# Side work between scores and maxima, and reciprocals on transposed blocks, in a two-layer attention and expert kernel

## The chip, the cores and the metric

The kernel runs on one core of one Trainium2 chip. The metric is the device time of one execution in microseconds (us); a comparison takes the median of several executions. The engines are named as in the profile: PE (TensorE; its weight loads are PEld), DVE (VectorE), ACT (ScalarE), POOL (GpSimd) and SP (SyncE, which only starts transfers here).

## What is computed

The reference is a stack of two layers on an input of 8 batches of 1024 rows of 128 numbers. Each layer has attention and then a mixture of experts, each behind a normalisation. Only the attention of layer 0, and the routing that prepares the experts of layer 0, are touched by the change:

```python
# layer 0: attention with 8 heads of 32, keys and values through a latent of 64
q = (x @ Wq.T).reshape(b, t, 8, 32)
kv_latent = x @ Wkv_down.T
k = (kv_latent @ Wk_up.T).reshape(b, t, 8, 32)
v = (kv_latent @ Wv_up.T).reshape(b, t, 8, 32)
scores = jnp.einsum('bqhd,bkhd->bhqk', q, k) * 32 ** -0.5
attn = jax.nn.softmax(scores, axis=-1)
out = jnp.einsum('bhqk,bkhd->bqhd', attn, v).reshape(b, t, 256) @ Wo.T
# layer 0: 14 experts of width 256, each row goes to its best two
probs = jax.nn.softmax(rows @ gate_w.T, axis=-1)
top2_p, top2_i = jax.lax.top_k(probs, 2)
...
```

Layer 1 (causal linear attention with 16 heads, 8 experts of width 512, one expert for each row) follows and is the same in both kernels.

## The kernel before

**Stages.** In the profiled execution the attention of layer 0 takes the time from about 52 us (first scores) to 1246 us. The experts of layer 0 follow until about 1423 us, then layer 1 until the end.

**Tiling.** The 8 heads are taken in two groups of 4, so there are 16 pairs n of batch and group. Each pair is cut into two blocks of 512 queries; there are 32 blocks. A block is worked off in 8 chunks of 128 keys (`kc`), and each chunk in two half steps (`hp` 0 and 1; `h` counts half steps over the whole stage). So there are 256 chunks.

**One chunk.** In the half step `hp` 0, `scores` makes the transposed scores of one chunk of keys for 512 queries and 4 heads: for each head a small matmul puts minus the row maximum into a bank of PSUM (line 398), the matmul of keys and queries adds the scores (line 399), and ACT takes the exponential of the bank (line 402). In the half step `hp` 1, `largest` makes untransposed scores of a later block (`LEAD` is 24 half steps, so 12 chunks ahead) for 4 heads (line 359), and DVE takes the negated maximum of each bank (line 363). `weigh` multiplies the exponentials of the chunk before with the values (line 414); it comes as two halves of 256 queries, one in each half step, except in the last chunks.

**Row sums.** The sums of the exponentials are gathered by POOL: it adds pairs of exponential tiles (line 228, a helper through which all pinned POOL work goes), and adds them into the tile `total`, partly by transfers that accumulate. Eight half steps after the end of a block, `add_up` sums `total` over the partitions with a matmul (line 424). `settle` then copies the sums to SBUF on ACT (line 435), and in eight pieces of 64 columns, one in each half step, DVE takes reciprocals (line 440) and POOL multiplies the weighed values with them (`outT<-nums,dens`).

**Maxima to rows.** `spread` reduces the maxima of a block (line 371), `spread_rows` transposes them on PE (line 376), splits them into three bf16 parts on DVE (lines 379 to 382) and sends them with 12 small transfers on SP's queue to the places where `scores` reads them.

**Banks.** All these matmuls but those of `weigh` write to one pool of 7 PSUM banks (`a_big`). A new tile takes the bank that came free first, in the order of the program. `weigh` has a bank of its own.

**Side work.** Between the two halves of the main work stand pieces for other batches: normalisation (`Norm`: `stats`, `power`, `offset`, `scaled`, `turned`), projections to queries and keys (`project`), `values`, and for finished batches `Finish`: the output projection, a normalisation, the routing `logits`, the steps of the choice of two experts (`first` to `weights`), `count` and `rank` of the rows, and `places`, after which 16 indirect transfers of each batch move its rows to the experts' regions (line 620, on POOL's queue). Lists give each piece its half step (`at(h, ...)`, in the dictionary `todo`). A piece stands behind the scores or the maxima of its half step, and in front of the half weighing:

```python
for piece in todo.pop(h):
    piece()
if weighing is not None:
    ...
        weigh(*weighing, half=hp)
```

**Order.** PE, DVE and ACT run their instructions in exactly the order in which the program issues them (`manual_schedule`), and POOL's pinned instructions as well. An engine that waits holds up all that stands behind it.

## Time and profile before

| what | value |
|---|---|
| median of 3 executions | 1997.78 us (1995.19 to 2002.73) |
| profiled execution, its own time | 2006.14 us |
| span of its trace, first to last instruction | 2003.8 us |
| mean granted PE clock | 0.964 |
| attention of layer 0 in the trace | about 52 to 1246 us |
| busy in 52 to 1246 us | PE 1166 us, DVE 896 us, POOL 905 us, ACT 665 us |

In a row of the groups, the name behind the line and the engine is the operation, then the tile written and the tiles read with their shapes, the number of instructions, and behind the bar the time in which at least one of them ran and the mean duration of one in ns. The last part is the time in which the engine idled in front of them, and what it waited for. A row of the timeline gives the start, the length, and how many instructions of a kind it merges (x8); in square brackets stands idle time in front of it. Matmuls of several heads overlap, so a merged row is longer than the distance to the next row's start; costs on PE are therefore taken from start to start. A row of windows gives the stretch, its length, then the busy time of PE, PEld, DVE, ACT and POOL, the granted clock and the DMA share.

### The profile page before, as it was taken

The page shows a single profiled execution, that of the slowest core. Times are in us where ns is not written, and L with a number is a line of the kernel's source. Part 1 is how long each engine was busy: PE and PEld are TensorE (multiplying, and loading weights), DVE is VectorE, ACT ScalarE, POOL GpSimd, SP SyncE. Part 2 cuts the span into 40 slices and gives each one's busy share as a digit, 9 for nine tenths or more (in the row PEclk, how much of TensorE's full clock was granted, in tenths as well). Part 3 has the DMA queues.
Part 4 walks back from the last instruction along what each step waited for, and adds up shares of the span by engine and source line. Part 5 has one row for each costly group of instructions (what it writes and reads, how often), then busy time and mean ns, then how long its engine had stood idle before and what let it go on. Part 6 is the DMA issues. An engine that isn't in the chain of part 4 may idle for free. (4 is left out here: it accounts for less than half of the span.)

```text
span 2003.8 us, 46295 instructions
## 1 busy us (share of the span) xinstructions
PE 1914.5 (96%) x17765; PEld 1010.4 (50%) x17765; DVE 1385.9 (69%) x3551; ACT 1083.1 (54%) x2338; POOL 1287.2 (64%) x1403
## 2 busy tenths in 40 slices
PE   8999999999999999999999998999599999998997
PEld 3333333333333333333333333699467777765897
DVE  6577778778778778778767785467457777754454
ACT  3455565564654565565565553366457666641443
POOL 1568668877778778778777884432545666624465
PEclk9999999999999999999999998999789999987999
DMA  5335345344344344444434441344222211101332
GB/s 154 64 79 108 70 86 110 71 95 100 83 92 102 83 88 99 91 88 96 93 78 102 98 96 72 135 132 134 81 71 87 79 50 51 51 23 54 108 106 63
DMA packets 64387, 176.41 MB, mean 88 GB/s; under 512 B 14889, under 2 KB 33776, under 8 KB 52512
## 3 DMA queue, kind: packets, MB, share of 16 engines
q0 software_dynamic: 30656, 136.45, 30.0%
q1 hardware_dynamic: 30112, 28.97, 5.2%
q10 hardware_dynamic: 3392, 7.95, 1.3%
q8 instruction: 143, 2.34, 0.5%
q14 instruction: 84, 0.69, 0.1%
HBM read 42.08 MB, written 35.96 MB: 39 GB/s over the span
## 5 line engine op out<-in xcount | busy, mean ns | idle before, releaser
L363 DVE TENSOR_REDUCE nmp<-big 128x1 f32<-128x512 f32 x1024 | 632.6, 680 | 248.9 <-PE big L359 248.8
L402 ACT ACTIVATE e<-st 128x512 f32<-128x512 f32 x1024 | 530.2, 603 | 379.3 <-PE st L399 303.8
L228 POOL TENSOR_TENSOR e<-e 128x512 f32<-128x512 f32 x364 | 452.3, 1288 | 8.1 <-PE num L414 7.8
L399 PE MATMUL st<-qT,kT 32*128 32x512 f32 x2048 | 340.6, 597 | 0.0
L414 PE MATMUL num<-e,v 128*32 128x256 f32 (+1 forms) x4040 | 332.0, 400 | 0.4 <-issue 0.3
L359 PE MATMUL big<-kT,qT 32*128 32x512 f32 x2048 | 320.1, 651 | 0.0
L414 PEld LDWEIGHTS num<-e,v 128*32 128x32 f32 x4040 | 81.1, 108 | 335.1 <-issue 304.6
L228 POOL TENSOR_TENSOR outT<-nums,dens 128x64 f32<-128x64 f32 x248 | 96.0, 510 | 168.2 <-DVE nm L371 99.5
L228 POOL TENSOR_TENSOR total<-e 128x512 f32<-128x512 f32 x124 | 154.7, 1320 | 46.3 <-ACT e L402 45.8
L1168 POOL DMA_INDIRECT got<-rows_out,found x128 | 125.8, 983 | 89.2 <-PE tp L1203 43.7
L399 PEld LDWEIGHTS st<-qT,kT 32*128 32x128 f32 x2048 | 154.8, 194 | 38.5 <-issue 33.0
L398 PE MATMUL st<-nb,ones_h 3*128 3x512 bf16 x1024 | 149.1, 389 | 11.0 <-DVE nmp L363 8.1
L359 PEld LDWEIGHTS big<-kT,qT 32*128 32x128 f32 x2048 | 102.1, 185 | 110.9 <-issue 46.9
L620 POOL DMA_INDIRECT rows_in<-xn,at x128 | 130.5, 1019 | 31.4 <-issue 30.9
L440 DVE RECIPROCAL dens<-dens 128x64 f32<-128x64 f32 x248 | 126.7, 531 | 4.5 <-ACT dens L435 4.5
L1717 POOL DMA_INDIRECT out_x<-y,to x72 | 79.1, 1098 | 67.4 <-DVE y L1715 53.4
L228 POOL DMA_DIRECT2D total<-e x91 | 84.4, 927 | 43.3 <-POOL e L228 23.9
L1698 ACT ACTIVATE g<-ph,wt 128x256 f32<-128x256 f32 x144 | 63.6, 474 | 85.3 <-PE ph L1695 85.3
L1016 POOL DMA_DIRECT2D rows_out<-y x68 | 39.4, 580 | 96.8 <-DVE y L1013 85.2
L398 PEld LDWEIGHTS <-ones_h 3*128 3x128 bf16 x1024 | 33.6, 91 | 128.3 <-issue 124.6
L1129 POOL TENSOR_TENSOR rs<-ve,mhalf 128x2 f32<-128x2 f32 x64 | 46.2, 722 | 80.1 <-DVE ve L1127 62.6
L1223 ACT ACTIVATE qm<-qk,cst 128x256 f32<-128x256 f32 x128 | 54.6, 496 | 53.6 <-DVE qk L1220 45.4
(289 smaller groups left out, 3064.5 us busy)
## 6 DMA issues: line engine op xcount, KB each, us to landing
total<-e POOLq DMA_DIRECT2D x91, 1024.0 KB
xr<-rows SPq DMA_DIRECT2D x36, 257.0 KB
xr<-rows_in SPq DMA_DIRECT2D x72, 128.0 KB
rows_out<-y POOLq DMA_DIRECT2D x68, 128.0 KB
nb<-part SPq DMA_DIRECT2D x384, 1.0 KB
blob<-in_blob ACTq DMA_DIRECT2D x8, 578.0 KB
blob<-in_blob SPq DMA_DIRECT2D x14, 321.0 KB
x<-in_x SPq DMA_DIRECT2D x8, 512.0 KB
```

The source lines that it names most:

```text
L228: return tc.keep_in_program_order(f(*args, **kw))
L359: nc.tensor.matmul(ps, lhsT=qTs[n][r, qc * P:(qc + 1) * P], rhs=kTs[n][r, kb * BLK:(kb + 1) * BLK], start=True, stop=True,)
L363: nc.vector.tensor_reduce(nmps[n][:, h, qc, kb:kb + 1], ps, AX.X, ALU.max, negate=True)
L398: nc.tensor.matmul(st, lhsT=ones_h[r3, :], rhs=nbs[n][r3, cols], start=True, stop=False)
L399: nc.tensor.matmul(st, lhsT=kTs[n][r, kc * P:(kc + 1) * P], rhs=qTs[n][r, cols], start=False, stop=True)
L402: nc.scalar.activation(e[:, h, :], st, AF.Exp, scale=SCALE0)
L414: nc.tensor.matmul(nums[n, qb][32 * h:32 * h + 32, cols], lhsT=vs[b][:, kc, c0:c0 + HD0], rhs=e[:, h, cols], start=kc == 0 and half != 1, ...
L440: nc.vector.reciprocal(s[:, cols], s[:, cols])
L620: ins = nc.gpsimd.indirect_dma_start(out=rows_in, out_offset=bass.IndirectOffsetOnAxis(ap=ats[k][:, j:j + 1], axis=0), in_=xn[:, c0 + j, : ...
L1168: ins = tc.keep_in_program_order(nc.gpsimd.indirect_dma_start(out=gots[p][:, i, k, :], out_offset=None, in_=rows_out, in_offset=bass.Indir ...
L1698: nc.scalar.activation(g[:, k, :], ps, AF.Relu, bias=w[:, L_B1 + k:L_B1 + k + 1])
L1717: ins = nc.gpsimd.indirect_dma_start(out=out_rows, out_offset=bass.IndirectOffsetOnAxis(ap=at[:, i:i + 1], axis=0), in_=y[:, i, :], in_off ...
```

## The change

1. The side work is divided in two: products of PE (`product`, in the dictionary `beside`) stand in the half step `hp` 0, behind the scores and in front of the maxima; what is left for DVE from them is run behind the maxima of the same chunk (`behind_maxima`). The functions `spread_rows`, `Finish.project`, `logits` and `rank` return their DVE part for this. ACT copies of projections, values and transposes stay with the product.
2. In a chunk with such a product, `weigh` comes as a whole behind the maxima; in the others it stays halved.
3. The half steps of all pieces are written anew (`frame`, `complete`, `last_half`); the output projection of a batch comes in 4 pieces of 2 chunks instead of 2 of 4; `places` is cut in two; the row sums come 11 half steps after the end of a block instead of 8.
4. `settle` no longer copies the sums. DVE transposes their 32x32 blocks straight from PSUM, takes 16 reciprocals for each partition, and transposes them back from a broadcast; POOL multiplies all 512 columns at once.
5. Two small copies of `counts` go from DVE to ACT for whole batches.

In the built order of the changed kernel, `counts<-ahead` stands on ACT in front of the exponentials of the next chunk.

```diff
         def spread_rows():
             ...
             nc.tensor.transpose(ps[:4 * CPK, :P], nm.rearrange("p h c -> p (h c)"), ident)
+            return lambda: spread_parts(n, qb, ps)
+
+        def spread_parts(n, qb, ps):
             parts = [stat0.tile([4 * CPK, P], BF16, name=f"part{i}") for i in range(3)]
...
-        def settle(n, qb, pieces):
+        def settle(n, qb):
...
-            out_b, top = outs[b, 0], tops.pop(0)
-            s = work.tile([P, BLK], F32, name="dens", bufs=1)
-            nc.scalar.copy(s, dens.pop((n, qb)))
-            w = BLK // pieces
-
-            def divide(i):
-                cols = slice(i * w, (i + 1) * w)
-                nc.vector.reciprocal(s[:, cols], s[:, cols])
+            out_b, top, den = outs[b, 0], tops.pop(0), dens.pop((n, qb))
+            few = stat0.tile([P, BLK // 32], F32, name="few")
+
+            def invert():
+                turned = work.tile([P, BLK // 32, 32], F32, name="dens", bufs=1)
+                nc.vector.transpose(turned.rearrange("p c d -> p (c d)"), den)
+                nc.vector.reciprocal(few, turned[:, :, 0])
+
+            def divide():
+                s = work.tile([P, BLK // 32, 32], F32, name="dens", bufs=1)
+                nc.vector.transpose(s, few.unsqueeze(2).to_broadcast([P, BLK // 32, 32]))
                 ins = pinned(
-                    nc.gpsimd.tensor_tensor,
-                    out_b[:, g, qb * BLK + i * w:qb * BLK + (i + 1) * w], top[:, cols], s[:, cols], ALU.mult,
+                    nc.gpsimd.tensor_tensor, out_b[:, g, qb * BLK:(qb + 1) * BLK], top,
+                    s.rearrange("p c d -> p (c d)"), ALU.mult,
                 )
...
+                self.copy = nc.scalar.copy if n == CPB else nc.vector.tensor_copy
...
-                nc.vector.tensor_tensor(xv, ps, xv, ALU.add)
+                return lambda: nc.vector.tensor_tensor(xv, ps, xv, ALU.add)
...
-                nc.vector.tensor_copy(self.both[:, :, 0], counts)
+                self.copy(self.both[:, :, 0], counts)
...
-                nc.vector.tensor_copy(counts, ahead[:, :, CPB])
+                self.copy(counts, ahead[:, :, CPB])
...
+        def frame(f):
+
+            h0 = 2 * CPB * 4 * f
+            if 1 <= f < NB - 1:
+                projections(2 * f + 1, h0, (0, 1, 4, 2))
+            if f == NB - 2:
+                projections(2 * f + 3, h0, (24, 26, 28, 30))
+            b = f + 2
+            if b < NB:
+                for i, k in enumerate((15, 16, 17, 23)):
+                    at(h0 + 2 * k + 1, measure, b, i)
+                at(h0 + 49, lambda b=b: prepared[b].power())
+            b = f + 1
+            if 2 <= b < NB:
+                at(h0 + 3, start_norm, b)
+                at(h0 + 3, lambda b=b: prepared[b].offset())
+                for i, k in enumerate((3, 4, 5, 6)):
+                    at(h0 + 2 * k + 1, lambda b=b, i=i: prepared[b].scaled(2 * i))
+                product(h0 + 14, turn_both, lambda b=b: prepared[b])
+                projections(2 * b, h0, (8, 11, 12, 14))
+                for i, k in enumerate((15, 17, 19, 25)):
+                    product(h0 + 2 * k, values, b, i)
+            if f:
+                complete(f - 1, h0)
+
+        def complete(b, h0):
+
+            f, norm = Finish(b, 0, CPB), []
+            for i, k in enumerate((3, 6, 9, 10)):
+                product(h0 + 2 * k, f.project, 2 * i, 2)
+            at(h0 + 13, lambda: norm.append(f.norm()))
+            for i, k in enumerate((7, 8, 10, 11)):
+                at(h0 + 2 * k + 1, lambda i=i: norm[0].stats(2 * i))
+            at(h0 + 23, lambda: norm[0].power())
+            at(h0 + 27, lambda: norm[0].offset())
...
+            product(h0 + (30 if last else 32), turn_both, lambda: norm[0])
+            product(h0 + (32 if last else 36), f.logits)
+            steps = (
+                (39, f.first), (39, f.exponentials), (45, f.second), (49, f.third), (51, f.fourth),
+                (51, f.exponential2), (53, f.count), (65, f.place, 0), (67, f.place, 1), (69, f.softmax),
+                (71, f.weights),
+            )
...
+        def settle_soon(h, n, qb):
+            invert, divide = settle(n, qb)
+            at(h + 1, invert)
+            at(h + 2 + h % 2, divide)
+
+        def summed(h, n, qb, e):
+            add_up(n, qb, e, True, True)
+            settle_soon(h, n, qb)
...
                     elif not quiet:
                         smax_step(h + LEAD)
-                    if spreading and h % HALVES == (HALVES + 1 - LEAD) % HALVES:
-                        spread_rows()
+                        for piece in behind_maxima:
+                            piece()
+                        behind_maxima = []
+                    if spreading and h % HALVES == (HALVES - LEAD) % HALVES:
+                        behind_maxima.append(spread_rows())
+                    products = beside.pop(h)
+                    if hp == 0:
+                        split = not products
+                    for piece in products:
+                        behind_maxima.append(piece() or (lambda: None))
...
-                        else:
+                        elif quiet or split:
                             weigh(*weighing, half=hp)
+                        elif hp == 1:
+                            weigh(*weighing)
...
-                                due[h + 8] = n, qb, total
+                                product(h + 11, summed, h + 11, n, qb, total)
```

## The prediction

> **What bounds the kernel now.** I read the page first (shares, slices), then the groups, then one frame by windows, then single chunks by the timeline. The page and two groups:
>
> ```profile
> span 2003.8 us, 46295 instructions
> PE 1914.5 (96%) x17765; PEld 1010.4 (50%) x17765; DVE 1385.9 (69%) x3551; ACT 1083.1 (54%) x2338; POOL 1287.2 (64%) x1403
> ...
> DVE  6577778778778778778767785467457777754454
> ...
> PEclk9999999999999999999999998999789999987999
> ...
> L363 DVE TENSOR_REDUCE nmp<-big 128x1 f32<-128x512 f32 x1024 | 632.6, 680 | 248.9 <-PE big L359 248.8
> ...
> L440 DVE RECIPROCAL dens<-dens 128x64 f32<-128x64 f32 x248 | 126.7, 531 | 4.5 <-ACT dens L435 4.5
> ```
>
> TensorE (PE) looks full, but its 96% hides waits: matmuls overlap, and one head of four that starts late costs time in a "busy" engine. Attention is 256 chunks from 52 to 1246 us, 4.66 us each; only it changes. The timeline of PE in a chunk without side work, then in a stalled one:
>
> ```profile
> 647.48 0.41 PE L398 MATMUL st<-nb,ones_h 3*128 3x512 bf16 x4
> 647.71 1.05 PE L399 MATMUL st<-qT,kT 32*128 32x512 f32 x8
> 648.69 0.64 PE L414 MATMUL num<-e,v 128*32 128x256 f32 x8
> 649.26 1.34 PE L359 MATMUL big<-kT,qT 32*128 32x512 f32 x8
> 650.52 0.64 PE L414 MATMUL num<-e,v 128*32 128x256 f32 x8
> 651.10 0.43 PE L398 MATMUL st<-nb,ones_h 3*128 3x512 bf16 x4
> ...
> 629.02 0.41 PE L398 MATMUL st<-nb,ones_h 3*128 3x512 bf16 x3
> 629.25 1.04 PE L399 MATMUL st<-qT,kT 32*128 32x512 f32 x6
> 631.52 0.37 PE L398 MATMUL st<-nb,ones_h 3*128 3x512 bf16 x1 [1.23 <-DVE nmp L363]
> ...
> 634.29 2.09 PE L359 MATMUL big<-kT,qT 32*128 32x512 f32 x8
> ```
>
> Start to start, scores take 1.21 us, each half of the weighing 0.57, maxima 1.26: 3.61. In the second chunk three heads of the scores start (x3) and the fourth 2.5 us later: it waits for a bank that VectorE (DVE) frees by a maximum. PE then loses its clock (maxima 2.09 long for 1.19) and the chunk takes 8.30. On DVE stood:
>
> ```profile
> 601.67 1.23 DVE L540 TENSOR_TENSOR cand<-cand,cst 128x112 f32<-128x112 f32 x1
> 602.83 0.54 DVE L440 RECIPROCAL dens<-dens 128x64 f32<-128x64 f32 x1
> 603.29 2.41 DVE L363 TENSOR_REDUCE nmp<-big 128x1 f32<-128x512 f32 x4
> ...
> L571 DVE COPY both<-counts x9: 160/619/2992, 314.0 to 1254.3; 128x14 f32<-128x14 f32 x9
> ```
>
> Between two sets of maxima lie routing steps and reciprocals; a copy of 14 elements takes 0.16 to 2.99 us, by what POOL does. So the bound is PE plus waits for banks. I call 32 chunks (64 half steps) a frame, k = 0 to 31. By windows, frame 4 is
>
> ```profile
> 637.00:788.00 151.00, 148.83 (x1292) 55.68 (x1288) 115.51 (x251) 85.82 (x170) 118.80 (x126) 0.99 0.44 92
> ```
>
> (PE, weight loads, DVE, ACT, POOL: DVE 76%, POOL 79%). Frames 1 to 5 run from 182.84 to 938.75 (first scores to first scores in the timeline), 151.2 us each. PE's own pieces of a frame, each without a wait, are 32 x (1.21 + 1.07) for scores and maxima, 36.0 for 64 half weighings, 26.1 for side work: 135. Some 16 us are waits, 9 of them in k = 20 to 31 (routing steps on DVE).
>
> **Part 1: side work between scores and maxima, weighing whole behind them.** A whole weighing in the tail takes 1.00 us (1204.78 to 1205.79) for 2 x 0.57: 0.14 saved where it is whole, 24 chunks of a frame, 3.3 us. But the banks (7, given out in the order in which they come free) set a new wait. With a side bank a chunk asks for 9, and its fourth maximum takes the bank of the second score. Exponentials begin 1.35 after the scores (647.48, first exponential 648.83), the first takes 0.60, the next end 0.48 later each: the second ends at +2.43. Maxima could start at 1.21 + 1.06 (a projection, 643.16 to 644.22) = +2.27, so they wait 0.2, as the plain chunk does for its first exponential (1.26 for 1.07). Kinds of chunk in the changed order:
> - 18 with one piece of about 1.05 us (6 projections, 4 values, 4 output projections of two chunks instead of 2 of four at 1.98, 4 row sums): 1.21 + 1.05 + 1.27 + 1.00 = 4.53; 81.6.
> - 2 with both transposes, 2 with spread transpose and projection (10 banks; the third exponential is waited for): 5.0 each; 20.1. Logits 1.21 + 1.81 + 1.07 + 1.00 = 5.09. Rank 0.63, waiting to +2.48: 4.55.
> - 2 with the spread transpose alone, weighing still halved, maxima waiting 0.5: 1.21 + 0.21 + 0.57 + 1.57 + 0.57 = 4.13; 8.3. 6 plain: 3.62; 21.7.
> Sum 141.3. Pieces drained by DVE are now drained behind the maxima, so the next scores wait for the second maximum instead of the first: 12 x 0.1 net = 1.2. That makes 142.5. What is late next is thus ACT's second exponential, no longer DVE.
>
> **Part 2: reciprocals.** Out: 8 x 0.46 (start to start) = 3.7 us of DVE per block of 8 chunks, ACT's copy of the sums (31 x 0.585 = 18 us, hidden in ACT's 46% idle), POOL's 8 products (96.0/31 = 3.1 us) and POOL's waits for them (168 us in all; hidden too, since POOL holds up exponentials for 13.6 us in all). In: two transposes of 128x512, one reciprocal 128x16 (0.2 by the 128x8 row, 203 ns), one POOL product 128x512 (1.28, as e<-e). The trace has no DVE transpose. Nearest rows: the 512-wide reduction, 0.60 start to start, and tensor_tensor 128x512, 0.69. I take 0.65. Ends: 0.60, and 2.4 (four bytes in four passes); nothing below[...]. So 1.5 for 3.7, in one place per block, behind the maxima of the chunk with the row sums. The gap that DVE has there until the next maxima is about 4.3 us from set to set, less 4 x 0.60: 1.9 on average (1.6 in front of a plain chunk), so 1.5 fits.
> At this place a rule could speak against the change. The row: the 128x14 SBUF copy takes 0.16 at best, 1.53 in the mean of frames 2 to 6, POOL being busy. If the second transpose (SBUF to SBUF) is held up so, 31 x 1.0 us come late, some 30 us, and the gain is gone. The Trainium skill, "SBUF — State Buffer", § Who interferes with whom, lists copy, cast and tensor_scalar as ops that take the port pair shared with GpSimd, and says that a DVE op with at most one SBUF input outside the 2-port modes does not contend. It doesn't name the transpose. I take the rule's zero, and keep 30 us for the range.
>
> **Part 3: routing, counts, moves.** The sums come 3 half steps later (11 for 8), so PE's waits for the landing of total (weighing 2.59 long at 134 us, 2.25 at 465) go. Routing steps are spread over more chunks. Left: the third step, 0.67 + 1.23 behind a plain chunk's maxima, where 3.6 less 4 x 0.60 leaves 1.2, so 0.7 too long; with others 1.0 per frame. The two copies of counts go to ACT (DVE 1.5 + 0.3 saved), but ACT is in order: counts<-ahead waits for the scan, which stands behind the maxima of k = 26 and the pair sum; it ends about 2.9 us into k = 27, whose exponentials, due at 1.35, queue behind it; the maxima wait for them: 1.9 per frame. Also off is moved from half step 26 to 27, in front of ACT's scaling in the same half step: the exponentials of k = 14 come 1.0 late: 1.0. The 16 indirect moves of a frame keep their pace (one per 4 half steps) and start 7 half steps later; on POOL they and the e sums pass one product instead of 8, and that product stands behind a full set of e sums (5 us), by when its transpose is done. Costed at nothing, hidden by POOL's 21% of slack; if that were gone, the place would cost POOL 1.3 for 3.1, still no loss. SP's 12 spread DMAs per block follow the same DVE steps, three and a half chunks before their use: nothing, and before that cover is gone they would have to land 15 us later.
> Frame: 142.5 + 1.0 + 1.9 + 1.0 = 146.4, for 151.2: -4.8, times 5 = -24. Frame 0 (130.4, no projections): -2. Frame 6 (153.4; four more pieces in k = 24 to 30, 3.7): -3. Frame 7 to the tail (86.8, by the same kinds 83.6): -3. Tail: -1. **Sum -33.** The profiled execution took 2006.1 (2003.8 in the span), so 1973; it lies 8 over the median 1997.8, so **1965**.
>
> **Rivals.** (a) Larger gain, about 1938: the 0.2 before each side chunk's maxima (18 x 0.2 x 6 = 22) doesn't appear, nor part of the ACT waits. For: before, chunks with side work had maxima of 1.07, no wait. Against: half a weighing stood there too.
> (b) No change, about 1994: ACT's late exponentials pass on to the next chunks (bank, maxima, DVE), 4 more per frame, or a second transpose held by POOL. For: the stall at 629 shows how one late DVE step takes two chunks and the clock.
> (c) Slower, 2039: transposing 4-byte values takes DVE several passes. At 2.0 us each the steps need 2 x 2.0 + 0.3 in a gap of 1.9: 31 x 2.4 = 74 lost, less 33, so 1998 + 41. It decides from 31 x (2T + 0.3 - 1.9) = 33, T = 1.3 us. For: no row. Against: DVE's other 512-wide ops are at 0.7.
> (d) That the change doesn't do what it says: the built order has one side piece in front of the maxima in 24 of 32 chunks and whole weighings behind, so no.
>
> **How the numbers follow.** 0.5% (10 us) is about what a measurement can tell from no change. Forecast 0.54 (own range 1948 to 1983), (a) 0.17, (b) 0.14, (c) 0.15: faster 0.71, same 0.14, slower 0.15. The range goes from half of (a) over (b): 1932 to 2006.
>
> **What would show it.** Right: 31 transposes of each kind at 0.6 to 0.7, RECIPROCAL 128x16 near 0.2; num matmuls 128x512 in three of four chunks; side chunks of 4.5 with maxima of 1.27; PE's waits on nmp gone from k = 20 to 31; an ACT wait of 2 us at counts<-ahead; PEclk without dips before 1180. Wrong: transposes over 1.3; scores over 2 us after each side chunk; side chunks of 4.33 (then (a)).

## The result: 9.5% slower, and the profile after

The changed kernel takes 2190.16 us (median of 4 runs, 2183.14 to 2195.32) where the kernel before takes 2000.25 on the same chip: a ratio of 1.095, 95% interval 1.090 to 1.100. The forecast was 1965 us, range 1932 to 2006. The profiled execution took 2195.29 us. From its page, then its groups of DVE:

```profile
span 2193.4 us, 43466 instructions
PE 2009.3 (92%) x16493; PEld 1032.1 (47%) x16493; DVE 1404.8 (64%) x3396; ACT 1066.0 (49%) x2321; POOL 1251.3 (57%) x1186
...
DVE  6565666767667767667666766457645767763454
...
PEclk9998999999998998899899997899968999996999
...
L363 DVE TENSOR_REDUCE nmp<-big 128x1 f32<-128x512 f32 x1024 | 636.3, 684 | 423.9 <-PE big L359 422.5
```

```profile
L297 DVE SCALAR_TENSOR_TENSOR off<-mv,rs 128x8 f32<-128x8 f32 (+1 forms) x18 | 33.8, 1877 | 1.8 <-POOL rs L228 1.8
L446 DVE STREAM_TRANSPOSE dens<-few 128x512 f32<-128x512 f32 x31 | 22.0, 711 | 1.0
L441 DVE STREAM_TRANSPOSE dens<-den 128x512 f32<-128x512 f32 x31 | 21.9, 706 | 0.0
L442 DVE RECIPROCAL few<-dens 128x16 f32<-128x16 f32 x31 | 7.9, 254 | 1.1
```

The transposes are close to what they were taken for (0.71 us for 0.65), so the way to a slower kernel that the prediction named is not the one taken. All engines are busy for a smaller share of the span than before; the clock row has its dips all over attention; DVE idles longer in front of the maxima (422.5 us for 248.8), waiting for PE. And one row stands out: `off`, a 128x8 step, takes 1877 ns on average, where the same line took 96 ns in attention before. A chunk with one piece of side work came out as forecast to the hundredth of a us. PE in one, by the timeline:

```profile
642.96 0.41 PE L401 MATMUL st<-nb,ones_h 3*128 3x512 bf16 x4
...
644.17 1.13 PE L334 MATMUL val<-wv_sb,xT 128*128 128x256 f32 x4
645.23 1.34 PE L359 MATMUL big<-kT,qT 32*128 32x512 f32 x8
646.49 1.07 PE L417 MATMUL num<-e,v 128*32 128x512 f32 x8
647.49 0.41 PE L401 MATMUL st<-nb,ones_h 3*128 3x512 bf16 x4
```

Start to start: scores 1.21, values 1.06, maxima 1.26, weighing 1.00, together 4.53 as forecast. The loss sits in a few chunks of each frame. (Chunk k is counted within the frame, k = 0 to 31, as in the list of half steps.) The windows' row of one frame, k = 0 to 31:

```profile
546.34:720.15 173.81, 158.98 (x1101) 57.35 (x1099) 121.34 (x230) 83.22 (x168) 115.34 (x99) 0.92 0.39 80
```

173.8 us for 151 before. Over an undisturbed chunk of their kind, k = 4 takes 5.6 us more, k = 14 7.6, k = 20 4.1, k = 27 6.6, k = 0 1.5 (up to 8.5 in other frames), and six more together 5.5. Without these 30.9 us the frame is 142.9; the prediction's sum without waits was 142.5. So the plan held, and the waits were missed. Three of them by the timeline, first k = 14 (DVE, POOL, PE and ACT):

```profile
621.60 4.93 POOL L228 TENSOR_TENSOR e<-e 128x512 f32<-128x512 f32 x4
621.68 4.88 DVE L297 SCALAR_TENSOR_TENSOR off<-mv,rs 128x8 f32<-128x8 f32 x1
622.84 1.12 PE L359 MATMUL big<-kT,qT 32*128 32x512 f32 x2
626.49 0.70 DVE L441 STREAM_TRANSPOSE dens<-den 128x512 f32<-128x512 f32 x1
626.60 0.88 ACT L310 ACTIVATE xn<-x,off,rs 128x128 f32<-128x128 f32 x2 [7.65 <-DVE off L297]
627.34 3.23 PE L359 MATMUL big<-kT,qT 32*128 32x512 f32 x6 [3.37 <-DVE dens L441]
```

`off` starts 0.08 us after POOL began four additions, and ends when the fourth is over. ACT, in order, has stood 7.65 us in front of `xn` with the exponentials behind it; PE had two of four maxima, stood 3.4 us, and goes on slowly: the granted clock is 0.57 up to 630.49 us and 0.50 after it, and the weighing behind takes 1.87 us for 1.00. Then k = 4:

```profile
566.89 4.92 POOL L228 TENSOR_TENSOR e<-e 128x512 f32<-128x512 f32 x4 [4.39 <-PE num L417]
568.50 0.89 DVE L570 TENSOR_TENSOR s<-p,p 128x8 f32<-128x8 f32 x1
569.43 1.19 DVE L571 TENSOR_SCALAR s<-s 128x8 f32<-128x8 f32 x1
570.65 0.20 DVE L572 RECIPROCAL s<-s 128x8 f32<-128x8 f32 x1
570.89 1.02 DVE L574 TENSOR_TENSOR shares<-p,s 128x8 f32<-128x8 f32 x2
571.83 0.17 DVE L371 TENSOR_REDUCE nm<-nmp 128x16 f32<-128x32 f32 x1
572.06 0.38 PE L376 MATMUL nmt<-cst,nm 128*16 128x128 f32 x1 [3.72 <-DVE nm L371]
572.23 1.92 PE L348 MATMUL prj<-xT,wk_sb 128*128 128x512 f32 x2
```

Five tiny steps of the weights (0.12 to 0.20 us each when alone) stand beside POOL's additions from 566.89 to 571.81 and take 3.4 us. The three that are late end when one of the additions does (additions end at 569.37, 570.59 and 571.81), and POOL goes on adding after the first two. `nm` stands behind them on DVE, PE's transposition of `nm` is now one half step nearer to it than before, and the projection after it runs at half clock (1.85 us start to start; 0.96 in k = 12 of this frame). Last k = 27:

```profile
688.52 4.95 POOL L228 TENSOR_TENSOR total<-e 128x512 f32<-128x512 f32 x4
688.95 4.67 DVE L529 TENSOR_TENSOR oh__6285<-cand,chosen 128x112 f32<-128x112 f32 x1
694.26 0.37 PE L401 MATMUL st<-nb,ones_h 3*128 3x512 bf16 x1 [2.21 <-DVE nmp L363]
```

The fourth step of the choice (0.27 us when alone) ends when POOL's four additions are over. The maxima stand behind it on DVE, and the fourth head of the scores waits for the bank that they free.

### The profile page after: what moved, and what is told of

It reads as the page before. It is cut to its first block, busy times and chain, and to the rows that moved or that the text cites. A ratio compares the mean times of both kernels' runs of the same rounds, so it can differ in the third digit from the quotient of the medians.

```text
span 2193.4 us, 43466 instructions
## 1 busy us (share of the span) xinstructions
PE 2009.3 (92%) x16493; PEld 1032.1 (47%) x16493; DVE 1404.8 (64%) x3396; ACT 1066.0 (49%) x2321; POOL 1251.3 (57%) x1186
## 5 line engine op out<-in xcount | busy, mean ns | idle before, releaser
L363 DVE TENSOR_REDUCE nmp<-big 128x1 f32<-128x512 f32 x1024 | 636.3, 684 | 423.9 <-PE big L359 422.5
L228 POOL TENSOR_TENSOR e<-e 128x512 f32<-128x512 f32 x364 | 450.0, 1267 | 309.2 <-PE num L417 308.7
L359 PE MATMUL big<-kT,qT 32*128 32x512 f32 x2048 | 372.4, 698 | 21.0 <-DVE dens L441 21.0
L402 PE MATMUL st<-qT,kT 32*128 32x512 f32 x2048 | 358.3, 617 | 0.0
L417 PE MATMUL num<-e,v 128*32 128x256 f32 (+1 forms) x2768 | 318.7, 533 | 1.8 <-issue 1.6
L359 PEld LDWEIGHTS big<-kT,qT 32*128 32x128 f32 x2048 | 123.3, 197 | 164.6 <-issue 96.8
L401 PE MATMUL st<-nb,ones_h 3*128 3x512 bf16 x1024 | 160.3, 401 | 35.3 <-DMA nb<-part 20.7
L417 PEld LDWEIGHTS num<-e,v 128*32 128x32 f32 x2768 | 57.9, 112 | 278.5 <-issue 259.6
L402 PEld LDWEIGHTS st<-qT,kT 32*128 32x128 f32 x2048 | 165.0, 201 | 36.5 <-issue 28.5
L310 ACT ACTIVATE xn<-x,off,rs 128x128 f32<-128x128 f32 x122 | 53.2, 505 | 63.2 <-DVE off L297 63.2
L1541 POOL DMA_INDIRECT rows<-row,where x64 | 64.0, 1000 | 29.4 <-issue 16.9
```

The costliest lines, as they stand in the source:

```text
L228: return tc.keep_in_program_order(f(*args, **kw))
L359: nc.tensor.matmul(ps, lhsT=qTs[n][r, qc * P:(qc + 1) * P], rhs=kTs[n][r, kb * BLK:(kb + 1) * BLK], start=True, stop=True,)
L363: nc.vector.tensor_reduce(nmps[n][:, h, qc, kb:kb + 1], ps, AX.X, ALU.max, negate=True)
L401: nc.tensor.matmul(st, lhsT=ones_h[r3, :], rhs=nbs[n][r3, cols], start=True, stop=False)
L402: nc.tensor.matmul(st, lhsT=kTs[n][r, kc * P:(kc + 1) * P], rhs=qTs[n][r, cols], start=False, stop=True)
L417: nc.tensor.matmul(nums[n, qb][32 * h:32 * h + 32, cols], lhsT=vs[b][:, kc, c0:c0 + HD0], rhs=e[:, h, cols], start=kc == 0 and half != 1, ...
```

## The experiments

Theory T, after this profile: a DVE step whose operands all lie in SBUF is held until POOL's run of four additions (5 us) is over, and what stands behind it makes PE stop and lose its clock. Rival R1: ACT's order (counts behind the scan, `xn` behind the offset) is the cause by itself. Rival R2: the whole weighing at a chunk's end makes POOL's additions, hence the tiles `e` and the exponentials, late (in front of its additions of `e`, POOL's waits for `num` rose from 7.8 to 308.7 us). Ratios are to the kernel before on the same chip. The changed kernel, run a second time, is the reference of the second group.

> The changed kernel itself, unedited, so that the edits beside it are read against it on the same chip: 1.095 of the kernel before, as in the first comparison (1.090 to 1.100), whatever the theory.

Measured: 1.087 (1.082 to 1.092), so 1.087 to 1.095 stands for the changed kernel in what follows.

**Four edits for T.** The main lines of each; with the first, the old call of `spread` at the end of the loop goes, with the second DVE's step in `offset`. The fourth edit is the three together.

```diff
# minimum first: directly behind smax_step, ahead of behind_maxima and todo
+                        if h % HALVES == (HALVES - 1 - LEAD) % HALVES:
+                            spread(*blocks[(h + LEAD) // HALVES])
# offset on POOL (minus: a tile of -1), behind the power
+                    pinned(nc.gpsimd.tensor_tensor, self.off, mvs[self.b][:, cs, 0], rstds[self.b][:, cs], ALU.mult)
+                    ins = pinned(nc.gpsimd.tensor_tensor, self.off, self.off, minus, ALU.mult)
# even chunks (only the entries that change)
-                (39, f.first), (51, f.fourth), (67, f.place, 1), (71, f.weights),
+                (41, f.first), (49, f.fourth), (65, f.place, 1), (73, f.weights),
-                at(h0 + 3, lambda b=b: prepared[b].offset())
+                at(h0 + 5, lambda b=b: prepared[b].offset())
```

> Edit: the minimum that closes a block's row maxima (nm, 0.18 us on DVE, every eighth chunk) is issued right behind its chunk's last maxima, ahead of the projection's addition and the side steps; everything else as in the changed kernel. Theory T (a DVE instruction whose operands are all in SBUF is held until POOL's run of four additions, about 5 us, is over; what stands behind it on DVE is late, and PE, having stood over 3 us, goes on at half clock): PE's transposition of nm no longer stands behind such steps, so the stalls of chunks 4, 12 and 20 of a frame (5.6 + 1.2 + 4.0 us over an undisturbed chunk) go, about 10 us in each of 6.5 frames: 2190 - 65 = 2125 us (2105 to 2145); chunks 14 and 27 stay as they are (12.2 and 11.2 us). Rival R1 (ScalarE's order is what costs: the normalisation behind the offset, the counts behind the scan): no change to these, 2180 to 2190. Rival R2 (whole weighing at the end of a chunk makes POOL's sums and with them the tiles e late): 2180 to 2190 too.

> Edit: the normalisation's offset (-mean x rs, 128x8) is made on POOL by two small products directly behind the power that makes rs, instead of on DVE; everything else as in the changed kernel. Theory T: the 4.9 us that DVE's offset stood goes, ScalarE's xn and the exponentials behind it are in time, chunk 14 of a frame falls from 12.2 to about 4.7 us: 7.5 us in each of 6 frames, 2190 - 45 = 2145 us (2130 to 2165); chunks 4, 20 and 27 stay. Rival R1 in its plain form (ScalarE waits because the offset is asked for a chunk too early, POOL's power itself being late behind the sums): rs and the offset come no earlier, and at most 2 us of the 7.5 go: 2175 to 2190. Rival R2: 2185 to 2190.

> Edit: five side steps with DVE instructions between SBUF operands are moved by one chunk, from behind an odd chunk (where POOL's four additions start) to behind an even one (where they are ending): first choice 39 to 41, fourth step 51 to 49, weights 71 to 73, second place 67 to 65, the early offset 3 to 5 (half steps of the frame); counts stay on ScalarE, and the later offset stays at 27. Theory T: chunk 4 falls by 5.6, chunk 20 by 4.0, chunk 27 by about 6, the second place by up to 2: 15 to 17 us in each of 6 frames, 2190 - 95 = 2095 us (2075 to 2120); chunk 14 stays at 12.2. Rival R1 (the counts on ScalarE are what holds chunk 27): chunk 27 stays at 11 us, and only 9 us a frame go: 2135. Rival R2: DVE's steps are not what matters, 2175 to 2190.

> Edit: the three edits together (minimum first, offset on POOL, side steps behind even chunks). Theory T: the stalls of chunks 4, 12, 14, 20 and 27 go, 22 to 25 us in each of 6 frames, and a frame comes to about 149 to 152 us: 2190 - 145 = 2045 us, less than the sum of the three single gains (since the first and the third share chunks 4 and 20), and still above the kernel before unless the chunks that were forecast shorter show it: 1990 to 2060. Rival R2 (the whole weighing): the exponentials still wait for tiles e, and the time stays above 2100.

Measured: minimum first 1.085 (1.080 to 1.091), offset on POOL 1.066 (1.062 to 1.070), even chunks 1.089 (1.085 to 1.093), all three 1.057 (1.054 to 1.060). Two of four gained next to nothing, and the sum fell short by half. The lengths of single chunks tell why (us, from the first scores of a chunk to those of the next, median of frames 1 to 6; k = 0 varies most, 8.5 in the second run of the changed kernel):

| kernel | ratio | k=0 | 4 | 8 | 14 | 20 | 24 | 27 |
|---|---|---|---|---|---|---|---|---|
| changed | 1.087 to 1.095 | 10.9 | 10.7 | 4.5 | 12.2 | 8.1 | 4.6 | 11.1 |
| minimum first | 1.085 | 11.7 | 5.0 | 4.5 | 13.0 | 4.3 | 9.6 | 9.5 |
| offset on POOL | 1.066 | 12.4 | 10.1 | 4.5 | 5.0 | 7.5 | 4.7 | 11.7 |
| even chunks | 1.089 | 11.7 | 5.0 | 7.7 | 12.2 | 4.3 | 11.1 | 5.9 |
| all three | 1.057 | 12.3 | 5.0 | 10.1 | 4.7 | 4.3 | 11.1 | 5.9 |
| rows early | 1.057 | 4.5 | 10.2 | 4.5 | 12.3 | 8.2 | 4.6 | 9.8 |
| short sums | 1.034 | 6.5 | 5.9 | 4.5 | 5.6 | 4.9 | 5.9 | 9.6 |
| changed, 3 row transfers | 1.065 | 4.5 | 10.9 | 4.5 | 12.2 | 8.1 | 4.7 | 11.1 |
| all, 3 row transfers, `to` and `at` on POOL | 0.989 | 4.5 | 5.0 | 4.5 | 4.5 | 4.3 | 4.6 | 3.6 |

Each edit took away the stalls that T gave it: k = 4 and 20 the first, k = 14 the second, k = 4, 20 and most of 27 the third. But k = 0 stayed slow, and k = 8 and 24, also first chunks of blocks, became slow (24 with the first edit, both with the third). There PE waits for the bias rows (the three small parts of each row maximum that `spread_rows` sends): the scores wait for a row 11 times in the changed kernel, 17 with the first edit, 24 with the third and 29 with all three. With the late steps gone, the block comes to its end before its successor's rows have landed. That is theory T2, which the next runs test.

```diff
# rows early: DVE splits the transposed minimum at once, ahead of the chunk's maxima
-                        behind_maxima.append(spread_rows())
+                        spread_rows()()
# all and rows: this, the three edits above, and
-                (65, f.place, 0), (65, f.place, 1)
+                (61, f.place, 0), (61, f.place, 1)
# halves
-                        elif quiet or split:
+                        elif True:
```

> Edit: the changed kernel, with the four DVE steps that make the bias rows (part, rest_m) issued at once behind PE's transposition, ahead of the chunk's maxima, where the kernel before had them, instead of behind these maxima. Theory T2 (new after the first four runs: the 12 row transfers are issued by SP one after another in about 9.6 us and land some us later; the steps behind the maxima start them 2 to 4 us later than before, while the four chunks that cover them have become shorter; so the first scores of a block wait for their rows, and the clock halves): the stalls of chunk 0 of a frame go, some 5 us at seven places of the span: 1.095 - 0.017 = about 1.078 of the kernel before (1.070 to 1.085); chunks 4, 14, 20 and 27 stay. Theory T alone (DVE held by POOL's runs of sums is the whole of it): chunk 0 has another cause, 1.090 to 1.100. Rival R2 (whole weighing): 1.090 to 1.100.

> Edit: the three edits together (minimum first, offset on POOL, side steps behind even chunks), with the bias rows early, and both places at half step 61 (chunk 30, even) instead of 65. Theory T with T2: of the three edits together, the stalls left were the first scores of a block in chunks 0, 8 and 24 of a frame (about 6, 6 and 7 us over an undisturbed chunk) and a place step in every other frame (7.5 us); they go, about 20 us in each of 6 frames, and 1.0566 of the kernel before becomes 0.985 (0.97 to 1.00). Theory T alone: the waits for rows stay, 1.04 to 1.057. Rival R2: over 1.03.

> Edit: the changed kernel, with every weighing in two halves again (0.57 us in each half step), behind the side products as before the change, instead of whole ones at the end of the side chunks. Theory T with T2: POOL's sums start no earlier, since the second half still ends the chunk; the same stalls, and two halves cost about 0.14 us more than a whole one in some 19 chunks of a frame: 1.095 to 1.11 of the kernel before. Rival R2 (whole weighing at the end of the chunk makes POOL's sums, and with them the tiles e and the exponentials, late): the waits of POOL's sums for the weighing fall from 309 us to near 10, and the time falls by 50 us or more: below 1.07.

Measured: rows early 1.057 (1.052 to 1.062), more than expected, with k = 0 at 4.5 in all six frames; all and rows 1.006 (1.003 to 1.009), above the expected range of 0.97 to 1.00; k = 27 still took up to 9.2 us; halves 1.106 (1.102 to 1.111). R2 falls: with two halves POOL still waits 296 us for `num`, the stalls are at the same chunks (10.2, 10.6, 7.3 and 10.3 us in k = 4, 14, 20 and 27), and the kernel is slower, as T said.

```diff
# rank later: all and rows, and
-                (53, f.count), (61, f.place, 0), (61, f.place, 1)
+                (53, f.count, False), (57, f.carry), (61, f.place, 0), (61, f.place, 1)
-            product(h0 + (43 if last else 54), f.rank)
+            product(h0 + (43 if last else 58), f.rank)
# counts on DVE, in the changed kernel
-                self.copy = nc.scalar.copy if n == CPB else nc.vector.tensor_copy
+                self.copy = nc.vector.tensor_copy
# short sums, in the changed kernel
-                        for i in range(4):
+                        for i in range(4 if quiet or kc == 1 else 1):
```

> Edit: the version of the last comparison (minimum first, offset on POOL, side steps behind even chunks, rows early, places at 61) with the rank's products four half steps later (58 for 54) and ScalarE's copy of the counts at half step 57 instead of right behind the scan at 53. Theory T with T2: the last large stall of a frame (chunk 27: 9.2 us; PE stood 2.2 us for both, which DVE gave 1.5 us late behind POOL's sums, and ScalarE's exponentials queued behind the counts) goes: 4.5 us in each of 6 frames, 1.0055 - 0.014 = 0.992 of the kernel before (0.985 to 0.998). If chunk 27 is slow for another reason, 1.003 to 1.008.

> Edit: the changed kernel, with the two copies of the counts on DVE again instead of ScalarE. Rival R1 (ScalarE in order behind the scan is what makes chunk 27 slow): its 11.2 us fall to 5, 6 us in each of 6 frames, 1.087 becomes 1.069. Theory T: DVE's fourth step, held 3.7 us by POOL, delays the maxima too, so PE waits for their banks in any case, and the copy on DVE may itself be held: 1.08 to 1.092.

> Edit: the changed kernel, with one instead of four of POOL's additions e + e in the chunks 3, 5 and 7 of a block (the other three heads' second addend is left out of the row sums); nothing else differs in order or place. Theory T: POOL's runs are 1.3 us instead of 5 in three of four places, DVE's steps between SBUF operands are held for at most that long there, and the stalls at the offset (chunk 14) and at chunks 4 and 20 go; the first scores of a block still wait for their rows, as in the three edits together: 1.087 becomes 1.05 (1.03 to 1.065). Rival R1 (order on ScalarE): 1.075 to 1.09, since POOL's power and the scan stand where they were.

(`carry` is the copy of the scan's last column to `counts`, which `count` then leaves out.) Measured: rank later 0.997 (0.994 to 0.999), k = 27 at 3.6; counts on DVE 1.099 (1.094 to 1.104), above T's range too, which ended at 1.092; short sums 1.034 (1.030 to 1.038). R1 falls: the counts' place on ACT is not what makes k = 27 slow (10.0 to 10.6 us in four of six frames with the copies on DVE), and with POOL's runs a quarter as long, k = 14 falls to 5.6 with ACT's order untouched. k = 27 stays at 9.6 there, since the additions beside it are those into `total`, which were left at four.

**The reciprocals alone.** In the kernel before, `settle` of the changed kernel, its two DVE steps in two consecutive half steps:

> Edit: the kernel before, with only the new reciprocals (two transposes and one 128x16 reciprocal on DVE in two consecutive half steps, one product of 512 on POOL, no copy of the sums by ScalarE) in the place of the eight pieces; order of the side work and whole weighings as before. Transposes of 0.71 us that POOL does not hold up, as in the changed kernel's trace: DVE loses 8 x 0.53 - 1.7 = 2.6 us of work per block, the stalls near chunks 20 to 27 shrink, and PE's own work stays: 0.99 of the kernel before (0.98 to 1.00). If the steps of 1.4 us in two places hold up the maxima there: 1.00 to 1.01.

Measured: 1.070 (1.066 to 1.075). Both expectations miss. The new DVE steps are not to blame (transposes 705 and 707 ns). Over all chunks attention is 138 us longer than before; the first chunks of the blocks (k = 0, 8, 16, 24) are longer by 145 us together, and the rest shorter by some 8. (Three times `at` is held 5.7 us in k = 30, a chunk that lost time before as well; k = 30 is longer by 14 us in all.) What PE's scores waited for, by the rows of the tile `nb`, first in this run, then in the kernel before:

```profile
L398 PE MATMUL st<-nb,ones_h x1024: 371/384/605, 52.0 to 1373.0; 3*128 3x512 bf16 x171
...
  DMA nb<-part: 52.8, 32
```

```profile
  DVE nmp L363: 8.1, 19
  DMA nb<-part: 2.7, 2
```

The waits for row transfers go from 2 to 32. The rows are issued at the same place in both programs. What differs is when POOL starts the 1 MB transfer that accumulates into `total`. Kernel before, SP's queue and POOL's around the last rows of block 14 (blocks counted from 0):

```profile
560.84 2.42 SPq L386 DMA_DIRECT2D nb<-part  x4
...
560.16 3.71 POOL L228 TENSOR_TENSOR e<-e 128x512 f32<-128x512 f32 x3
564.17 0.93 POOL L228 DMA_DIRECT2D total<-e  x1 [0.30 <-POOL e L228]
```

With the reciprocals alone, one block earlier, and PE's scores behind it (in block 14 it is alike: the accumulation is 1.54 us ahead, and the chunk takes 13.0 us):

```profile
571.03 3.10 SPq L386 DMA_DIRECT2D nb<-part  x5
...
572.38 0.92 POOL L228 DMA_DIRECT2D total<-e  x1 [0.30 <-POOL e L228]
...
577.64 0.37 PE L398 MATMUL st<-nb,ones_h 3*128 3x512 bf16 x1 [0.78 <-ACT e L402]
577.86 1.02 PE L399 MATMUL st<-qT,kT 32*128 32x512 f32 x2
579.56 0.37 PE L398 MATMUL st<-nb,ones_h 3*128 3x512 bf16 x1 [0.69 <-DMA nb<-part]
```

Before, the last of 12 rows is issued by 563.26, the accumulation 0.9 us after it, and the scores from 564.75 on do not wait. With the new reciprocals the accumulation goes out at 572.38, 1.75 us ahead of the end of the last row's issue (574.13), and the fourth head's row is there at 579.56, 5.4 us after it. The packets of the DMA engines in the trace tell what happened between: before, the last row's packets are through at 563.99, and the accumulation's run from 565.67 to 570.25; here the accumulation's run from 573.86 to 579.27, and the packets of the last two rows, 16 small ones, lie among them, from 576.44 to 577.20 and from 578.32 to 579.11. Over the blocks 1 to 30: in the kernel before the accumulation follows the last row by 0.3 to 3.3 us in 29 (one has it 2.8 us ahead, and stalls at 84 us); with the reciprocals alone it is ahead by 0.1 to 3.7 us in 29; in the changed kernel ahead by 0.2 to 2.8 us in 12, nine of which stall, and no other does. That POOL is earlier because it no longer waits for eight pieces is inferred: its waits in front of `outT` fall from 168.2 to 5.0 us, but no run held POOL's transfer back alone. Sending the rows in 3 transfers takes some 3.2 us of SP's queue instead of 9.6, so that they are out 6 us or more ahead of the scores:

```diff
             for i in range(3):
-                for h in range(4):
-                    row = 32 * h + i
-                    nc.sync.dma_start(out=nbs[n][row:row + 1, ...], in_=parts[i][CPK * h:CPK * (h + 1), :])
+                nc.sync.dma_start(out=nbs[n].rearrange("(h r) t -> h r t", r=32)[:, i, ...], in_=parts[i])
```

> Edit: the kernel before with only the new reciprocals, and the bias rows of a block sent by 3 transfers (one for each part, 4 rows of 4 x 128) instead of 12. Theory T2 in its sharper form (what makes the rows late is that POOL's 1 MB accumulation, now earlier because POOL makes one product instead of eight, is issued ahead of the last rows): the last rows go out some 6 us earlier, ahead of the accumulation, the waits of the first scores go, and 1.07 becomes 0.99 of the kernel before (0.98 to 1.00). If the loss has another cause (the steps on DVE, POOL's longer product): 1.06 to 1.075.

> Edit: the changed kernel with the bias rows in 3 transfers instead of 12, issued at the same place. Theory T2: the stalls of chunk 0 go, as with the rows early (1.0567 there), and DVE's steps stay held by POOL's sums in chunks 4, 14, 20 and 27: 1.057 (1.045 to 1.07). If the order of issue does not matter: 1.08 to 1.095.

> Edit: the version with the rank later (minimum first, offset on POOL, side steps behind even chunks, rows early, rank's products at 58, counts copied at 57), with the bias rows in 3 transfers, and the target rows of the moves (to, at) made on POOL by small products and sums instead of on DVE, where they were held 5.5 us in two of six frames. Theory T with T2: frames 4 and 5 fall from 156.5 to 148 us, and the others stay at 148 or below: 0.9967 - 0.008 = 0.988 of the kernel before (0.98 to 0.995). If the POOL steps delay POOL's sums: 0.995 to 1.005.

> Edit: the kernel before, with the bias rows in 3 transfers instead of 12; the control. Theory T2: its rows are ahead of the accumulation in 30 of 31 blocks already, one stall of 2.5 us at the start goes: 0.995 to 1.00 of the kernel before. If twelve issues are a burden in themselves (SP, descriptors), 0.98.

Measured: reciprocals alone 0.985 (0.981 to 0.989), where with 12 rows it was 1.070; changed kernel 1.065 (1.061 to 1.069); all 0.989 (0.986 to 0.992); the control 0.993 (0.990 to 0.996), slightly better than expected. No scores wait for a row transfer in the first two. One edit of a transfer that lies on no busy engine moves the reciprocals alone by 8.5% and the kernel before by 0.7%: T2, that the scores wait for their rows, is shown. The edit gives the rows more time as well as another order; that it was the accumulation that delayed them rests on the blocks and packets above. The windows' rows of one frame of the first and of the third:

```profile
609.10:753.00 143.90, 143.24 (x1292) 54.68 (x1289) 103.89 (x229) 83.14 (x166) 112.19 (x95) 1.00 0.43 89
```

```profile
618.10:765.50 147.40, 144.80 (x1108) 53.06 (x1104) 109.75 (x224) 82.73 (x168) 117.69 (x111) 1.00 0.46 94
```

Both keep the full clock. In frames without a long hold the old order of the side work with the new reciprocals (143.9) is shorter than the new order mended (147.4). Over the frames 1 to 5 they are even, 147.3 and 147.4, since two frames of the old order are longer (below), and the intervals of the two kernels overlap: neither order is shown to be better. In the new one some 6 us of waits are left, in k = 21, 24 and 28 to 30 (5.9, 4.6, 5.5, 6.2 and 4.4 us), where POOL holds up DVE's splitting of the rows and the second step of the choice.

In two of six frames the best of these still lost 9 us: in one (152.4 us) `at` was held for 5.69 us, in the other (152.9) the copy `counts<-ahead` for 5.34. The last run takes the steps `to` and `at` from DVE:

```diff
-                    nc.vector.scalar_tensor_tensor(to, chosen[...], float(UNIT * REG0), mine, ALU.mult, ALU.add)
-                    nc.vector.tensor_scalar(ats[k][:, :n], to, float(TW0), None, ALU.add)
+                        pinned(nc.gpsimd.tensor_tensor, to, chosen[:, k, b, :], region, ALU.mult)
+                        pinned(nc.gpsimd.tensor_tensor, to, to, mine, ALU.add)
+                        pinned(nc.gpsimd.tensor_tensor, to, to, head, ALU.add)
+                        pinned(nc.gpsimd.tensor_copy, ats[k], to)
```

> Edit: the kernel before with the new reciprocals and the bias rows in 3 transfers (0.9853 of the kernel before), and the target rows of the moves (to, at) made on POOL by small products and sums instead of on DVE. Theory T: the two frames of 152.5 and 152.9 us fall to the 143.8 of the others, 9 us each, and nothing else moves: 0.9853 - 0.009 = 0.976 of the kernel before (0.970 to 0.982). If the frames differ for another reason: 0.983 to 0.99.

Measured: 0.982 (0.979 to 0.985): 1932.63 us for 1969.14, the best of all versions, but no certain step beyond 0.985. The frame held at `at` recovers (143.6 us). The one held at the copy does not (151.4), as its step was not moved, and the copy is caught in one more frame (150.8 for 143.8). DVE in this one, then POOL:

```profile
441.93 5.32 DVE L594 COPY counts<-ahead 128x14 f32<-128x14 f32 x1
442.01 5.24 DVE L367 TENSOR_REDUCE nmp<-big 128x1 f32<-128x512 f32 x4
444.41 2.85 DVE L442 STREAM_TRANSPOSE dens<-den 128x512 f32<-128x512 f32 x1
...
441.29 0.98 POOL L633 DMA_INDIRECT rows_in<-xn,at  x1 [0.17 <-issue]
442.28 4.93 POOL L232 TENSOR_TENSOR e<-e 128x512 f32<-128x512 f32 x4
```

The copy of the counts, still on DVE in this kernel, is caught, and the maxima behind it with it. So taking single steps from DVE does not end the holds as long as others of their kind stay beside POOL's additions.

## Why the prediction was wrong, step by step

**Right:** the kinds of chunk in Part 1 (4.53 each for the side chunks, 5.01 and 5.02 for the transposes, 5.16 for the logits where 5.09 was forecast, 3.60 to 3.62 plain) and their sum; T in Part 2 (0.71 for 0.65) and the reciprocal of 16 (0.25 for 0.2); the rule's zero for the second transpose, 711 ns in the mean while POOL is busy beside it. The reciprocals do gain: 0.985 once their side effect is mended, of which the three transfers alone make 0.993.

**Failed, Part 3: "Left: the third step ... with others 1.0 per frame" and "the exponentials of k = 14 come 1.0 late".** The prediction had the row before it: a 14-element copy of 0.16 to 2.99 us "by what POOL does". It used this, in the mean, for the second transpose alone; the steps that it moved it priced by their own length, and did not ask where POOL's runs stand to their new places. The list before was `hs = (36, 38, 37, 42, 46, 50, 47, 54, 56, 58, 62, 66)`: all DVE steps in even half steps, between scores and maxima. The new list has them in odd ones, behind the maxima, and several behind odd chunks, at whose end POOL starts its run. Summed over DVE's instructions in attention that took over 0.3 us more than the shortest of the same line and shape, the excess is 42 us before and 112 us after; the largest is 2.8 us before and 4.9 after. Single terms: `off` and `xn` 7.6 us for 1.0; the fourth step with the scan and the counts 6.6 for 1.9 (and by the run with the counts on DVE not for the reason given, the counts' place); the weights and the first step in front of `nm`, 5.6 and 4.1 for nothing. The Trainium skill, "SBUF — State Buffer", § Who interferes with whom, cited there only for the transpose, also says that two SBUF inputs contend with GpSimd's reads, and that the later one waits for the whole instruction. The trace agrees on who is held. On how long it is not of one kind: the weights in k = 4 were let in behind one addition, as the page has it, but `off` behind none of the first three, only behind the fourth (4.88 us).

**Failed, Part 3: "SP's 12 spread DMAs ... nothing, and before that cover is gone they would have to land 15 us later".** Of the three and a half chunks, some 9.6 us go into twelve issues one after another. What was left before was 1.5 us in the block at 563 (last issue 563.26, scores from 564.75) and 5.3 in the one at 637 (636.61, 641.96), and the end of the issue is not when a row lands: with the accumulation ahead it took 5.4 us more. The rows that would have told were the timeline of SP's queue beside POOL's, which the prediction did not read.

**Failed, Part 2: "POOL's waits for them (168 us in all; hidden too ...)", costed at nothing.** That POOL became faster was not free: as far as the orders of issue tell, those waits were what kept its 1 MB transfer behind the rows. "DMA: Bandwidth & Descriptors", § Issuing engines are not separate DMA queues, of the Trainium skill says that transfers of all engines run on the same 16 DMA engines and interleave. The trace agrees: the packets of the late rows lie among those of the accumulation.

**Rival (b)** had the right shape ("one late DVE step takes two chunks and the clock") but not the size: it priced 4 us a frame, and the stalls cost 31. PE's standing still is only part of a stall: of the 7.6 us in k = 14 it stood for 3.4; the clock cost about 0.9 in the weighing alone (1.87 for 1.00), and the six maxima after the pause took 3.15 us for 0.80, where clock and waits are not separated. Rival (c) named DVE's transposes, which T = 0.71 excludes.

**Two readings** in the prediction are off, without weight for its sum. The rows under "On DVE stood" are from 601 to 605 us; in the stalled chunk at 629 us DVE ran the last steps of the places and reciprocals. And its frames begin one chunk early: 182.84 us is the first score of chunk 31, that of chunk 32 comes at 186.47.

## What to carry to other kernels

When a step is moved, look up what the other engines do at its new place, and price it by the longest row of its kind, not the mean: a DVE step between SBUF operands can cost as much as POOL's longest run without a gap (here up to 4.9 us for four additions). When an engine is relieved, list what it will now start earlier, and put these starts beside the small transfers that something on the critical path waits for. If an edit removes the stall that it was made for and the time stays, look for the chunk that became slow instead; two waits in turn hide each other.

## What was not expected of the hardware

- Which DVE steps are held by POOL's additions: with two SBUF inputs (`off` 4.88 us for 0.16, `oh` 4.67 for 0.27), and with one SBUF input `at` (5.7 for 0.17, with the reciprocals alone), the copy of the counts (5.3 for 0.17, in the last run) and the cast of a row part (1.38 for 0.21). Not held themselves: maxima from PSUM, `STREAM_TRANSPOSE` from PSUM and from SBUF (706 and 711 ns), reciprocals (0.20 us amid the additions in k = 4), and the batch statistics (0.30 us at most).
- A hold can outlast single instructions, but need not. In the changed kernel's attention DVE was held for over 0.3 us in 61 steps. Six of `off` and four of `oh` came in only behind POOL's fourth addition; 21 steps, those of the weights among them, came in behind one addition while POOL went on adding. What decides between the two is open. `counts<-ahead` began 0.35 us before the additions did, while POOL was starting an indirect transfer, and was held as well.
- A 1 KB row issued 1.2 us after a 1 MB accumulation was there 5.4 us after the end of its issue.
